# First attention stage: V's projection behind the penalties, product with V one slot later, earlier reciprocals, an end without slots

## The chip, the cores and the metric

The kernel runs on one NeuronCore of a Trainium2 chip. Its engines work side by side, each through its own queue in order: TensorE (PE in the profile; its weight loads are PEld), VectorE (DVE), ScalarE (ACT), GpSimd (POOL) and SyncE (SP), which issues most of the transfers. They wait for each other by semaphores. PE writes its results to PSUM, from where DVE or ACT copy them to SBUF.

The metric is the device time of one execution in microseconds (us). Before the change the median of three runs is 2411.57 us (2407.48 to 2413.13).

## The reference

The input is x, 4 sequences of 512 tokens with 128 features, all in float32. The first stage, the only one that the change touches, is one causal attention layer with 16 heads of 64; `x` here has gone through a layernorm without weights, and the result is added to the input:

```python
q = (x @ Wq).reshape(b, s, HEADS, HEAD_DIM)
k = (x @ Wk).reshape(b, s, HEADS, HEAD_DIM)
v = (x @ Wv).reshape(b, s, HEADS, HEAD_DIM)
scores = SCALE * jnp.einsum('bqhd,bkhd->bhqk', q, k)
causal = jnp.triu(jnp.ones((s, s), dtype=x.dtype), k=1)
scores = scores + MASK_PENALTY * causal
attn = jax.nn.softmax(scores, axis=-1)
out = jnp.einsum('bhqk,bkhd->bqhd', attn, v).reshape(b, s, HEADS * HEAD_DIM)
return out @ Wr
```

The penalty is -50, not minus infinity, so every score counts. The second stage is a second layernorm and six layers of windowed attention and a gated feed-forward block; its result is added too.

## The kernel before

Everything is kept transposed: features on the 128 partitions, the 512 tokens of a sequence along the free axis. The second stage starts at about 631 us of the profiled execution and isn't touched.

The first stage goes through 128 "rows" (class `Rows`): for each sequence `b` (4), each pair of heads `c` (8, as `NC`), and each tile `t` of 128 queries (4). The order of the instructions is the order in which the program issues them (`manual_schedule`). A loop over *slots* `m` (L321) handles two rows per slot, so two slots, an even and an odd one, make one pair of heads. A slot works on `now`, its two rows, and on `old`, the two rows of the slot before. For a row:

- `scores` (L216): 8 matmuls of Q by K into a PSUM tile `sc` of two banks; there are two such tiles, so a row takes the one that the same row of the last slot had.
- `penalty` (L229): adds the mask to the tile by a matmul with an identity in bf16.
- `maximum` (L241, DVE): the negated row maxima of both heads.
- `exponents` (L247, ACT): two activations that also give the row sums `den`; they read `sc` and so set it free.
- `inverse` (L256, DVE): the reciprocals of `den`, 128x2. `normalise` (L259, POOL): multiplies the probabilities by them.
- `transposes` (L270): a slot later, four PE transposes per head into a bank `pt` (two of them); head 0 is copied out by ACT (L274), head 1 by DVE (L276), to `pT1`, a tile for one pair of heads with two buffers.

Between these stand the projections. `make_q` (L180, copied out by ACT, L182) comes in even slots, `make_k` (L186, copied out by DVE, L188) in odd ones, both for the next pair of heads. `make_v` (L195, copied out by DVE, L202) makes one token tile of V for 8 heads; it stands in odd slots (28 of 32, of which slot 1 makes three, and slot 0 makes two). All of them, the layernorm steps (L93, L102, L110) and `project_out1` (L302) write the one PSUM bank `pj`, so each waits until the one before it has been copied out.

`times_v1` (L287) multiplies V by the transposed probabilities of one pair of heads, in two halves of four matmuls, into the one bank `o1`; after the second half DVE copies it out (L297, `aT`). In the kernel before, slot `m` begins with a half for the pair `(m - 3) // 2`: the first half in odd slots, the second in even ones. The probabilities that the first half reads were transposed and copied in the slots up to the one just before.

`project_out1` (L302, 8 matmuls, added to the input by DVE in L303) of a sequence follows in the second slot pair of the next sequence. The layernorm steps of the next sequence (`norm_x`: mean, var, scale) and of the stage's results (`norm_x1`) are put at the end of 18 of the even slots. The var step ends in a chain of small DVE operations (L104, L79 to L85).

The last slots run with no rows: the loop goes to `last + 5`, that is 64 slots with rows and 5 that hold only what is left (transposes, products with V, the last output projection).

Of the kernel before, what the change touches and what calls it, by code (L numbers as in the profile page):

```python
# [20 lines left out]
NC = INNER // P  # L21
# [10 lines left out]
def body(ctx: ExitStack, tc: tile.TileContext, a, out: bass.AP):  # L32
# [7 lines left out]
    B, S, _ = x.shape  # L40
    L = a["wqkv"].shape[0]
    NT = S // P
# [79 lines left out]
    def norm_x1(bank, b):  # L122


        def out_():
            xT[b] = new_xT()
            return xT[b]

        return layernorm_steps({}, bank, lambda: x1T[b], out_)


    with tc.tile_pool(name="s1", bufs=1) as s1, tc.tile_pool(
# [20 lines left out]
        def bank1():  # L153
            return ps1.tile([P, 512], F32, tag="pj", name="ps_pj", bufs=1)
# [13 lines left out]
        def norm_x(b):  # L168
            def out_():
                xnT[b] = s1.tile([P, S], F32, tag="xnT", name="xnT", bufs=2)  # L170
                return xnT[b]

            return layernorm_steps({}, bank1, lambda: x0T[b], out_)
# [16 lines left out]
        def make_v(b, j, t):  # L190

            if t == 0:
                vs[b, j] = s1.tile([P, NT, 512], F32, tag="v1", name="v1", bufs=3)
            p = bank1()
            mm(  # L195
                p,
                lhsT=xnT[b][:, t * P : (t + 1) * P],
                rhs=wv[:, j * 512 : (j + 1) * 512],
                start=True,
                stop=True,  # L200
            )
            nc.vector.tensor_copy(vs[b, j][:, t, :], p)  # L202
# [75 lines left out]
        def times_v1(b, c, half):  # L278

            if half == 0:  # L280
                os_[b, c] = ps1.tile([P, S], F32, tag="o1", name="ps_o1", bufs=1)
            o = os_[b, c]
            for k in (2 * half, 2 * half + 1):
                for h in range(2):
                    col = (2 * c + h) % HEADS * HD
                    j, col = col // 512, col % 512
                    mm(  # L287
                        o[h * HD : (h + 1) * HD, :],
                        lhsT=vs[b, j][:, k, col : col + HD],
                        rhs=pTs[b, c][:, h, k, :],  # L290
                        start=(k == 0),
                        stop=(k == NT - 1),
                        skip_group_check=True,
                    )
            if half == 1:
                at = aTs[b, c] = s1.tile([P, S], F32, tag="aT1", name="aT1", bufs=NC + 2)
                nc.vector.tensor_copy(at, o)  # L297

        def project_out1(b):
            y = bank1()  # L300
            for c in range(NC):
                mm(y, lhsT=wr[:, c, :], rhs=aTs.pop((b, c)), start=(c == 0), stop=(c == NC - 1))  # L302
            nc.vector.tensor_tensor(x1T[b], y, x0T[b], ALU.add)  # L303
# [12 lines left out]
        make_k(0, 0)  # L316

        last = len(rows) // 2  # L320
        for m in range(last + 5):  # L321
            b, c, odd = m // (2 * NC), m // 2 % NC, m % 2
            now = rows[2 * m : 2 * m + 2]
            old = rows[2 * m - 2 : 2 * m] if m else []

            g = (m - 3) // 2
            if 0 <= g < B * NC:
                times_v1(g // NC, g % NC, 1 - odd)
            for r in now:
                r.scores()  # L330
            for r in now:
                r.penalty()
            if now:
                now[0].maximum()
            if old:
                old[0].transposes()
            if now:
                now[0].exponents()
                now[1].maximum()

            bn, cn = (b, c + 1) if c + 1 < NC else (b + 1, 0)
            if bn < B:
                (make_k if odd else make_q)(bn, cn)
            if old:
                old[1].transposes()
            if now:
                now[1].exponents()
                now[0].inverse()
                now[0].normalise()
            if m < 2:  # L350
                make_v(0, 0, 2 * m)
                make_v(0, 0, 2 * m + 1)
            if odd and c < NT and b < B:
                make_v(b, 1, c)
            elif odd and c >= NT and b + 1 < B:
                make_v(b + 1, 0, c - NT)
            if now:
                now[1].inverse()
                now[1].normalise()
            if not odd and 1 <= c <= 3 and b + 1 < B:  # L360
                if c == 1:
                    norms[b + 1] = norm_x(b + 1)
                norms[b + 1][c - 1]()
            if b > 0 and c == 1 and odd:
                project_out1(b - 1)
                norms1[b - 1] = norm_x1(bank1, b - 1)
            if b in range(1, B) and not odd and 4 <= c <= 6:
                norms1[b - 1][c - 4]()


    s2 = ctx.enter_context(tc.tile_pool(name="s2", bufs=1))
# [518 lines left out]
```

## Time and profile before

| what | value |
|---|---|
| median of three runs | 2411.57 us |
| the profiled execution as timed | 2416.6 us |
| its span, first to last instruction | 2414.8 us |
| first score matmul of slot 0 | 27.21 us |
| end of the last output projection of the first stage | 630.6 us |
| mean granted PE clock | 0.992 |
| PE busy from 300 to 400 us | 89.48 us of 100 |
| DVE, ACT, POOL busy there | 56.49, 43.65, 38.01 us |

The span is taken in the same profiled execution as the rows that the prediction uses. PE is the engine that is busy longest in both stages. A row of the timeline gives the start in us, the length in us, the engine, the line and operation, the tile written and the tiles read, and in square brackets the idle time of the engine just ahead of it with what ended it. Matmuls of float32 count twice in the number of instructions (128x512 x2 is one projection). Matmuls are pipelined, so the next one often starts before the row's end.

### The profile page before, as it was taken

To read this page: it belongs to the slowest core of one execution; us is meant where nothing else is said; L and a number is where in the kernel's file an instruction comes from. 1 tells how busy PE (TensorE), PEld (TensorE's weight loads), DVE (VectorE), ACT (ScalarE), POOL (GpSimd) and SP (SyncE) were. 2 spreads that over 40 slices of the span, in tenths; PEclk is the share of its full clock that TensorE was granted. 3 is DMA by queue.
4 is the path that set the end of the run, shared out by engine and by line. 5 is a ranking of instruction groups with operands and counts; after the bars stand their busy time and mean duration, and the time that the engine had idled before them with its cause. 6 is when DMAs were issued, how large, how long until landed. Compare 5 with 4: busy or idle time off the path is not lost.

```text
span 2414.8 us, 81635 instructions
## 1 busy us (share of the span) xinstructions
PE 2230.5 (92%) x35056; PEld 1446.4 (60%) x35088; DVE 1697.1 (70%) x2692; ACT 1300.6 (54%) x2166; POOL 1435.9 (59%) x1897
## 2 busy tenths in 40 slices
PE   6888989889788999999999999999999999999997
PEld 3555555555356666666666666666666666666664
DVE  3655555646577777777777777778787777877874
ACT  2444444445244655656665555665556656655662
POOL 1443443434476767667767667677667677666660
PEclk9999999999899999999999999999999999999999
DMA  3000000000122233222332223222232223322220
GB/s 108 1 1 1 1 1 1 1 1 1 36 59 65 57 85 78 55 71 61 86 73 58 68 62 85 68 66 64 65 88 63 65 69 78 81 59 67 65 58 15
DMA packets 91027, 125.82 MB, mean 52 GB/s; under 512 B 25263, under 2 KB 39469, under 8 KB 90669
## 3 DMA queue, kind: packets, MB, share of 16 engines
q1 hardware_dynamic: 90236, 119.02, 20.1%
q8 instruction: 280, 4.59, 0.9%
q10 hardware_dynamic: 432, 1.57, 0.2%
q14 instruction: 79, 0.64, 0.1%
HBM read 20.41 MB, written 1.05 MB: 9 GB/s over the span
## 4 chain that ended last, share of the span: by engine, by line
PE 58%; DVE 11%; issue 3%; ACT 2%; POOL 0%; ACTq 0%; POOLq 0%
PE ps_proj L436 19%; PE ps_one L532 10%; PE ps_one L627 7%; PE ps_att L602 6%; PE ps_att L570 5%; PE ps_proj L660 2%; PE ps_proj L661 2%; PE ps_proj L674 2%; DVE on L612 2%; DVE yt L79 1%; DVE rot L457 1%; DVE t L461 1%; ACT vt L514 1%; PE ps_att L559 1%; PE ps_one L93 1%
## 5 line engine op out<-in xcount | busy, mean ns | idle before, releaser
L436 PE MATMUL ps_proj<-wqkv,xs 128*128 128x512 f32 x1152 | 570.5, 618 | 31.6 <-ACT vt L514 22.9
L472 POOL TENSOR_TENSOR rot<-rot,t 128x1024 f32<-128x1024 f32 x192 | 453.4, 2361 | 196.8 <-DVE t L461 194.9
L259 POOL TENSOR_TENSOR pr<-pr,den 128x1024 f32<-128x1024 f32 x128 | 239.9, 1894 | 375.5 <-DVE den L256 375.5
L447 ACT ACTIVATE sq<-ps_proj 128x1024 f32<-128x1024 f32 x192 | 196.9, 1025 | 408.5 <-PE ps_proj L436 370.5
L480 POOL TENSOR_TENSOR rot<-rot,ss 128x1024 f32<-128x1024 f32 x192 | 365.4, 1903 | 15.1
L436 PEld LDWEIGHTS ps_proj<-wqkv,xs 128*128 128x128 f32 x1152 | 199.5, 191 | 219.9 <-issue 157.3
L452 DVE TENSOR_REDUCE ss<-sq 128x16 f32<-128x1024 f32 x192 | 233.1, 1214 | 54.0 <-ACT sq L447 53.2
L241 DVE TENSOR_REDUCE nm<-ps_sc 128x2 f32<-128x1024 f32 x128 | 156.0, 1219 | 124.4 <-PE ps_sc L229 124.4
L274 ACT COPY pT<-ps_pt 128x512 f32<-128x512 f32 x128 | 75.1, 587 | 300.6 <-PE ps_pt L270 300.6
L457 DVE TENSOR_TENSOR rot<-ps_proj,lt 128x1024 f32<-128x1024 f32 x192 | 233.5, 1216 | 0.0
L461 DVE TENSOR_TENSOR t<-ps_proj,lt 128x1024 f32<-128x1024 f32 x192 | 232.9, 1213 | 0.0
L627 PEld LDWEIGHTS ps_one<-aT,wo 128*128 128x128 f32 x1536 | 186.3, 192 | 45.3 <-issue 44.5
L82 POOL TENSOR_TENSOR yt<-y 128x32 f32<-128x32 f32 x288 | 69.3, 241 | 241.5 <-DVE y L80 226.5
L532 PE MATMUL ps_one<-ident,rot 128*128 128x128 f32 x1536 | 211.2, 281 | 1.2 <-ACT qT L535 0.6
L580 DVE TENSOR_REDUCE mx<-ps_att 128x16 f32<-128x1024 f32 x96 | 117.5, 1224 | 120.2 <-PE ps_att L570 120.2
L247 ACT ACTIVATE pr<-ps_sc,nm 128x512 f32<-128x512 f32 x256 | 175.2, 696 | 23.1 <-DVE nm L241 23.0
L627 PE MATMUL ps_one<-aT,wo 128*128 128x128 f32 x1536 | 187.3, 275 | 0.4 <-ACT aT L535 0.4
L532 PEld LDWEIGHTS ps_one<-ident,rot 128*128 128x128 f32 x1536 | 165.8, 142 | 20.4 <-issue 2.8
L611 DVE RECIPROCAL rden<-ps_att 128x8 f32<-128x8 f32 x192 | 39.5, 206 | 195.9 <-PE ps_att L602 190.8
L602 PEld LDWEIGHTS ps_att<-vw,pT 64*32 64x32 f32 x9216 | 105.3, 105 | 109.4 <-issue 76.6
L602 PE MATMUL ps_att<-vw,pT 64*32 64x65 f32 x9216 | 129.9, 224 | 37.8 <-DVE on L612 28.2
L514 ACT COPY vt<-ps_proj 128x512 f32<-128x512 f32 x192 | 103.1, 589 | 85.6 <-PE ps_proj L436 84.6
(127 smaller groups left out, 4063.5 us busy)
## 6 DMA issues: line engine op xcount, KB each, us to landing
vw<-vt SPq DMA_DIRECT2D x1152, 65.0 KB
vw_first<-vt SPq DMA_DIRECT2D x336, 65.0 KB
wqkv<-in_wqkv_dram SPq DMA_DIRECT2D x18, 512.0 KB
wo<-in_wo_dram SPq DMA_DIRECT2D x6, 512.0 KB
w<-in_w_dram SPq DMA_DIRECT2D x6, 341.0 KB
xr<-in_x_dram SPq DMA_DIRECT2D x4, 256.0 KB
out_dram<-tmp_t SPq DMA_DIRECT2D x4, 256.0 KB
w<-in_w_dram SPq DMA_DIRECT2D x12, 64.0 KB
```

The lines of the kernel that those rows point to most:

```text
L247: nc.scalar.activation(self.pr[:, h, :], self.sc[:, h, :], AF.Exp, bias=self.nm[:, h : h + 1], accum_out=self.den[:, h : h + 1],)
L259: nc.gpsimd.tensor_tensor(self.pr, self.pr, self.den.unsqueeze(2).to_broadcast([P, 2, S]), ALU.mult)
L436: mm(p[:, c, :], lhsT=u.xs[:, u.T * P : (u.T + 1) * P], rhs=wpart[j][:, c * 512 : (c + 1) * 512], start=True, stop=True,)
L447: nc.scalar.activation(u.sq, u.p[j], AF.Square)
L452: nc.vector.tensor_reduce(u.ss[:, j * HEADS : (j + 1) * HEADS], heads(u.sq), AX.X, ALU.add)
L457: nc.vector.tensor_tensor(heads(t0), heads(pf), lt[:, u.T, 2 * j].unsqueeze(1).to_broadcast([P, HEADS, HD]), ALU.mult)
L461: nc.vector.tensor_tensor(t1.rearrange("p (h t d) -> p h t d", t=2, d=half), pf.rearrange("p (h t d) -> p h t d", t=2, d=half)[:, :, ::-1, :],
L472: nc.gpsimd.tensor_tensor(u.r[j], u.r[j], u.t1, ALU.add)
L480: nc.gpsimd.tensor_tensor(heads(u.r[j]), heads(u.r[j]), u.ss[:, j * HEADS : (j + 1) * HEADS].unsqueeze(2).to_broadcast([P, HEADS, HD]), AL ...
L532: nc.tensor.transpose(tp[:, c * P : (c + 1) * P], src[:, (4 * g + c) * P : (4 * g + c + 1) * P], ident)
L602: mm(o[j * W : (j + 1) * W, h, c * (HD + 1) : (c + 1) * (HD + 1)], lhsT=u.pT[h * HD : (h + 1) * HD, 4 * g + c, j * W : (j + 1) * W], rhs=u ...
L627: mm(y[:, 0:P], lhsT=wo_w[0][:, c, :], rhs=u.aT[:, c, :], start=(c == 0), stop=(c == NC - 1))
```

## The change

It reorders the loop and nothing else; every instruction of the first stage is still issued, as often as before.

```diff
-        for m in range(last + 5):
+        for m in range(last + 1):
...
-            g = (m - 3) // 2
-            if 0 <= g < B * NC:
-                times_v1(g // NC, g % NC, 1 - odd)
+            if m >= 4:
+                g = m // 2 - 2
+                times_v1(g // NC, g % NC, odd)
             for r in now:
                 r.scores()
             for r in now:
                 r.penalty()
             if now:
                 now[0].maximum()
+            if m < 2:
+                make_v(0, 0, 2 * m)
+                make_v(0, 0, 2 * m + 1)
+            if odd and c < NT:
+                make_v(b, 1, c)
+            elif odd and b + 1 < B:
+                make_v(b + 1, 0, c - NT)
             if old:
                 old[0].transposes()
...
             if bn < B:
                 (make_k if odd else make_q)(bn, cn)
+            if now:
+                now[0].inverse()
+                now[0].normalise()
             if old:
                 old[1].transposes()
             if now:
                 now[1].exponents()
-                now[0].inverse()
-                now[0].normalise()
-            if m < 2:
-                make_v(0, 0, 2 * m)
-                make_v(0, 0, 2 * m + 1)
-            if odd and c < NT and b < B:
-                make_v(b, 1, c)
-            elif odd and c >= NT and b + 1 < B:
-                make_v(b + 1, 0, c - NT)
-            if now:
                 now[1].inverse()
                 now[1].normalise()
...
+        times_v1(B - 1, NC - 2, 1)
+        for half in range(2):
+            times_v1(B - 1, NC - 1, half)
+        project_out1(B - 1)
```

- V's projection is issued behind the penalties of the slot's two rows, ahead of the transposes and of K's projection. The bank `pj` then goes from Q (slot before) to V to K; before, it went from Q to K to V. On DVE the copy of V moves to directly behind the first row's maximum, ahead of the copy of the first row's transposes.
- The halves of the product with V come one slot later: the first half in even slots, the second half, and with it the copy L297, in odd ones.
- The first row's reciprocal and normalisation are issued ahead of the second old row's transposes. On DVE that puts the reciprocal ahead of that row's copy L276.
- The five slots without rows become one (for the last transposes), and what is left of the products with V and the last output projection is written out behind the loop.

## The prediction

> **What bounds the kernel now.** I began with the page: busy shares, then the 40 slices. The first stage fills the first ten slices (up to about 625 us of 2414.8); only there does the change reorder work.
>
> ```profile
> PE 2230.5 (92%) x35056; PEld 1446.4 (60%) x35088; DVE 1697.1 (70%) x2692; ACT 1300.6 (54%) x2166; POOL 1435.9 (59%) x1897
> ...
> PE   6888989889788999999999999999999999999997
> ```
>
> TensorE (PE) is the busiest engine, and in the first stage its digits are mostly 8 and 9: no room but its own waits. So the second view is what PE waited for between 60 and 600 us (columns: engine, tile and line <- releaser: us in all, times, longest).
>
> ```profile
> PE ps_pj L195 <- DVE k L188: 25.5, 27, 1.1
> PE ps_o L287 <- ACT pT L274: 10.7, 12, 0.9
> PE ps_pt L270 <- DVE pT L276: 6.2, 6, 1.0
> PE ps_sc L229 <- issue: 4.6, 29, 0.2
> ...
> PE ps_pj L302 <- DVE v L202: 2.3, 3, 0.8
> ```
>
> Two waits carry it: V's projection (L195) for K's copy out of the single `pj` bank, in 27 odd slots; and the product with V (L287) for the ScalarE copy of the last transpose, in 12 even slots. The third view is the timeline of one odd slot (from 94.10) and one even slot (from 102.98).
>
> ```profile
> 94.10 2.00 PE L216 MATMUL ps_sc<-k,q 64*128 64x256 f32 x16
> ...
> 96.37 1.04 PE L270 MATMUL ps_pt<-ident,pr 128*128 128x128 f32 x8
> ...
> 96.46 1.22 DVE L241 TENSOR_REDUCE nm<-ps_sc 128x2 f32<-128x1024 f32 x1 [2.18 <-PE ps_sc L229]
> ...
> 97.25 1.02 PE L186 MATMUL ps_pj<-xnT,wk 128*128 128x512 f32 x2
> ...
> 98.11 1.04 PE L270 MATMUL ps_pt<-ident,pr 128*128 128x128 f32 x8
> ...
> 99.33 0.68 DVE L188 COPY k<-ps_pj 128x512 f32<-128x512 f32 x1
> ...
> 100.06 1.13 PE L195 MATMUL ps_pj<-wv,xnT 128*128 128x512 f32 x2 [0.92 <-DVE k L188]
> ...
> 101.12 1.94 PE L287 MATMUL ps_o<-pT,v 128*64 128x512 f32 x8
> ...
> 102.98 2.00 PE L216 MATMUL ps_sc<-k,q 64*128 64x256 f32 x16
> ...
> 107.42 1.04 PE L270 MATMUL ps_pt<-ident,pr 128*128 128x128 f32 x8
> ...
> 108.69 0.59 ACT L274 COPY pT<-ps_pt 128x512 f32<-128x512 f32 x1
> ...
> 109.34 1.08 PE L287 MATMUL ps_o<-pT,v 128*64 128x512 f32 x4 [0.89 <-ACT pT L274]
> ```
>
> Read starts: K's projection ends at 98.27, yet its copy starts at 99.33, because VectorE (DVE) is busy with a maximum; L195 is held to 100.06. An odd slot with V takes 102.98 - 94.10 = 8.88 us. Scores follow L287 by 1.87 (101.12 to 102.98), so the even slot ends at 111.21: 8.23 us.
>
> **The change, part by part.** Times below count from a slot's first score matmul.
>
> *V's projection behind the penalties (27 odd slots after the first pair).* No instruction is added. Without V and without a wait an odd slot takes 6.85 (timeline: L216 at 591.89, L270 594.16, L186 595.04, L270 595.90, L287 596.87, L216 598.74). One projection takes the queue 0.86 (L186 to L270). So: V at 2.27, first transposes 3.15, K 4.03, second transposes 4.9, product 5.9, next scores 7.72 if nothing waits. K now needs V's copy out of the bank. DVE: row maximum 2.36 to 3.58; the next DVE work starts 1.14 after a maximum starts (302.81 to 303.94), so V's copy runs 3.50 to 4.18 (0.68; V itself ends at 3.39); a PE consumer follows a copy's end by 0.05 (99.33 + 0.68 to 100.06). K starts at 4.24: a wait of 0.21 takes the place of 0.92. The slot takes 7.94, a gain of 0.94. Queued behind K are the second transposes and the next slot. Bounds: wait 0 (gain 1.16) to 0.92 (gain about 0.25); I take 0.21 since every duration in it has a row.
>
> The transposes come 0.88 later, and ScalarE (ACT) copies them before its exponents: copy 3.75 to 4.34, first row's exponents to 5.8 (1.45 each row), second row's 6.26 to 7.7. The next slot's second row of scores, which needs that PSUM back, starts at 7.94 + 0.95: 1.2 us cover. GpSimd (POOL) normalises 6.9 to 10.65 (3.75 for two rows); the next slot transposes these rows at 10.6 and 12.4, while they are ready at 8.8 and 10.65: 1.8 us cover.
>
> Of these 27 slots five follow a slot that computes a variance, whose chain of small operations holds DVE:
>
> ```profile
> 75.13 1.82 DVE L80 TENSOR_SCALAR y<-yt 128x4 int32<-128x4 int32 x1
> ...
> 79.25 1.22 DVE L241 TENSOR_REDUCE nm<-ps_sc 128x2 f32<-128x1024 f32 x1
> ```
>
> L80 takes 0.17 at 13.16, where POOL is idle, and 1.82 here: it ends at 76.95 as POOL's normalisation does (73.18 + 3.75). The maximum starts at 3.78 instead of 2.36. After the change the early reciprocal lets POOL end 0.33 sooner, but the copy of the finished product (L297, 0.60) moves into odd slots, ahead of the maximum: maximum 4.13, V's copy ends 5.94, K 6.0, second transposes 6.86, next scores 9.59, against 10.30 before (75.47 to 85.77). Gain 0.71. Three slots go on to the output projection (L302): it waited 0.78 for V's copy, and will wait about as long for K's (K ends 5.26, copy 5.97 to 6.65). Before, scores to scores 16.81 (197.34 to 214.15); after 6.7 + 7.06 + 1.87 = 15.63, gain 1.18.
> Sum: 19 x 0.94 + 5 x 0.71 + 3 x 1.18 = 25.0.
>
> *Product with V one slot later.* The two buffers of transposed probabilities allow it: the second half is issued ahead of the transposes that refill its buffer. In 12 even slots without a layernorm step L287 then follows the second transposes by 0.97 (595.90 to 596.87) rather than 1.92 (107.42 to 109.34): 12 x 0.95 = 11.4. The last even slot (598.74 to 606.84) gains about 1.1. In the 18 slots with a layernorm step that step hid the copy: nothing. Bounds: 10.7 (PE's listed wait alone) to 12.5; I take 12.5, as starts include the weight reload.
>
> *Early reciprocals.* An instruction of 0.15 is moved ahead of a copy; if it must wait, the copy L276, the second reciprocal and the next maximum queue behind it. Even slot (scores at 307.60): DVE ends the second maximum at 5.59 (311.97 + 1.22), the sums are ready at 5.34 (312.74 + 0.20): cover 0.25. Odd: 6.6 against 5.8. So it costs nothing; without cover it delays DVE, not yet PE, whose transposes need that bank 3 us later. What POOL gains lies behind its 2 us of cover, except the 0.33 above.
>
> *Start and end.* Slots 0 and 1 issue two and three V projections in a row, each waiting for the copy before it, and the second maximum queues behind these copies. The second row's exponents end at about 50.3, K's copy at 49.2; slot 2 scores at 49.3 and 50.4 (before 49.05 and 50.0), slot 3 at 56.4 (before 57.85), since it has no product yet. That 1.4 gain is owed at the end: one more product half (1.94) behind the last transposes, and a wait of about 0.85 for L297 that slots used to hide, with all of the projection queued behind it; POOL starts 0.5 sooner. I get 16.8 to 18.5 from the last slot's scores to L302 (before 606.85 to 623.46 = 16.61), middle a loss of 1.0. In the four last odd slots, without V, the one behind a variance loses 0.3. Together 0; bounds -2 and +2.
>
> **Sum:** 25.0 + 12.5 = 37.5 us. The profiled execution: 2414.8 span (2416.6 as timed) becomes 2377.3 (2379.1). It lies 5 us above the median shown, 2411.57, which becomes 2374.
>
> **Rivals.**
> *The wait only moves (0.20).* `pj` stays a single bank, written by Q or K and V in turn. If V's copy comes 0.7 later than I place it (another DVE item ahead), K waits 0.9: 27 x 0.7 = 19 of the 37.5 go, time 2393. For: the maximum stands directly ahead of that copy. Against: V is ready at 3.39, before the maximum is done.
>
> *The clock holds (0.10).* Two of the six slots behind a variance lost half of PE's clock.
>
> ```profile
> 284.00:286.00 2.00, 0.81 (x5) 0.95 0.00 0
> 286.00:288.00 2.00, 2.00 (x4) 0.50 0.00 0
> ```
>
> (Columns: window, length, PE busy and count, granted clock, DMA.) There two waits of 1.04 and 1.07 came within 3 us, and the stretch at half clock after such waits cost 1.65 (L195 + L287 take 1.19 + 3.52 at 230.26, 1.13 + 1.94 at 100.06). With one wait of 1.8 in their place these may go, and one at the end: 3.3 to 5, time about 2370.
> The Trainium skill (TensorE: Matmul & The Clock Gate, "What's actually happening") has the clock fall after an idle window of about 3.4 us; here 2.1 us of waits in pieces were enough, so the rows are stricter than that rule. By the rule alone no slot would fall, and the time would be about 2370.
>
> *The clock falls in every odd slot: slower (0.04).* If K's new wait, with what follows it, reaches some 2.1 us in 4, each of 27 odd slots pays 1.65: 45 lost against 37.5 won, time 2419. It decides from the point at which 23 of 27 fall. Against: 22 such slots with a wait of 0.92 kept a granted clock of 1.00, and I count 0.21.
> The skill's same page ("A second HAM failure mode: psum-queue depth-cycling") tells of such small idles between PSUM banks making the clock swing; it speaks against this change, but the trace's ordinary odd slots, with longer waits of that kind, don't show it.
>
> *It doesn't do what it says (0.04).* Another wait of the same size ends last in each slot, such as the second row's scores for their PSUM (cover 1.2 in odd and 0.6 in even slots): gain near 0, time 2411. Nothing in the listed waits points there.
>
> **How the numbers follow.** Forecast 0.62, the others as above. What the measurement can tell from no change is about 0.2%, 5 us. Faster: 0.62 + 0.20 + 0.10 = 0.92; the "no" case gives same 0.03 and, with the falling clock, slower 0.05. The range runs from 2364 (every wait bound at its best, the clock whole, and 4 us of spread between runs) to 2394 (the moved wait).
>
> **What would show it.** L195 should wait for nothing in the steady slots, and L186 appear waiting for the V copy L202 with about 0.2 each, some 5 in all. L287's wait for L274 should be gone from the even slots. Odd slots of 7.9 and even ones of 7.3, 15.2 a pair against 17.1. L256 should wait no longer for L247 than before. Wrong: L186's waits near 0.9, scores waiting for exponents (L247), or granted clocks of 0.5 in ordinary odd slots.

## The result, and the profile after

The changed kernel takes 2372.97 us (median of 4 runs, 2370.81 to 2376.22) against 2412.35 us (4 runs, 2407.48 to 2417.58): ratio 0.9838, 95% interval 0.9814 to 0.9861. The forecast was 2374, its range 2364 to 2394. The profiled execution has a span of 2371.3 us, 43.5 less than before. At the addition that ends the first stage (L303) 39.7 of these have been won: 630.63 before, 590.91 now. The other 3.8 came about in the second stage, which isn't touched; the four runs of either kernel differ by more than that.

The page of the changed kernel, PE's share and its slices:

```profile
PE 2222.6 (94%) x35056; PEld 1448.1 (61%) x35088; DVE 1696.8 (72%) x2692; ACT 1301.6 (55%) x2166; POOL 1436.9 (61%) x1897
...
PE   6999999998789999999999999999999999999997
```

The same instructions fill more of a shorter span; the gain is in the first ten slices, where digits of 8 became 9. What PE waited for between 60 and 575 us:

```profile
PE ps_pj L186 <- DVE v L202: 9.1, 5, 1.8
PE ps_sc L229 <- issue: 4.8, 30, 0.2
...
PE ps_pj L302 <- DVE k L188: 1.5, 3, 0.5
PE ps_pt L270 <- DVE pT L276: 1.4, 1, 1.4
```

The 25.5 us of V's projection (L195) and the 10.7 of the product (L287) are gone. What came in their place is K's wait for V's copy, 9.1 us in five slots only, those behind a variance. An odd slot (from 90.28) and an even one (from 98.31) of the timeline:

```profile
90.28 2.00 PE L216 MATMUL ps_sc<-k,q 64*128 64x256 f32 x16
...
92.55 1.08 PE L195 MATMUL ps_pj<-wv,xnT 128*128 128x512 f32 x2
...
93.47 1.04 PE L270 MATMUL ps_pt<-ident,pr 128*128 128x128 f32 x8
...
93.78 0.68 DVE L202 COPY v<-ps_pj 128x512 f32<-128x512 f32 x1
...
94.52 1.13 PE L186 MATMUL ps_pj<-xnT,wk 128*128 128x512 f32 x2
...
95.48 1.04 PE L270 MATMUL ps_pt<-ident,pr 128*128 128x128 f32 x8
...
96.45 1.94 PE L287 MATMUL ps_o<-pT,v 128*64 128x512 f32 x8
...
98.31 2.00 PE L216 MATMUL ps_sc<-k,q 64*128 64x256 f32 x16
...
102.75 1.04 PE L270 MATMUL ps_pt<-ident,pr 128*128 128x128 f32 x8
...
103.71 1.94 PE L287 MATMUL ps_o<-pT,v 128*64 128x512 f32 x8
...
105.58 2.00 PE L216 MATMUL ps_sc<-k,q 64*128 64x256 f32 x16
```

K's projection starts at 4.24 in its slot (94.52 - 90.28), 0.06 after V's copy ends. The odd slot takes 8.03 us (8.88 before), the even one 7.27 (8.23 before). K's small wait isn't in the list of waits, because the modelled end of the transposes ahead of it (93.47 + 1.04) reaches up to it; only the starts show it.

Slot lengths from the starts of L216, summed over the first stage from the first score to L303 (603.42 before, 563.77 after):

| where | won, us |
|---|---|
| 19 odd slots with V, 0.855 each | 16.2 |
| 3 odd slots that go on to the output projection | 3.4 |
| 5 odd slots behind a variance: 3 x 0.46, 2.11, 2.07 | 5.6 |
| 12 even slots without a layernorm step, 0.955 each, and the last one, 1.14 | 12.6 |
| slots 0 to 2 | 2.4 |
| odd slot behind the last variance, and the end | -0.6 |
| sum | 39.6 |

### The profile page after: what moved, and what is told of

It is laid out like the page before. It is cut to its first block, busy times and chain, and to the rows that moved or that the text cites. A ratio compares the mean times of both kernels' runs of the same rounds, so it can differ in the third digit from the quotient of the medians.

```text
span 2371.3 us, 81682 instructions
## 1 busy us (share of the span) xinstructions
PE 2222.6 (94%) x35056; PEld 1448.1 (61%) x35088; DVE 1696.8 (72%) x2692; ACT 1301.6 (55%) x2166; POOL 1436.9 (61%) x1897
## 4 chain that ended last, share of the span: by engine, by line
PE 77%; DVE 14%; issue 3%; ACT 3%; POOL 1%; DMA 1%; SPq 0%; ACTq 0%; POOLq 0%
PE ps_proj L439 19%; PE ps_one L535 10%; PE ps_one L630 7%; PE ps_att L605 6%; PE ps_att L573 6%; PE ps_sc L216 5%; PE ps_o L287 4%; PE ps_pt L270 3%; PE ps_proj L663 3%; PE ps_proj L664 3%; PE ps_proj L677 2%; DVE on L615 2%; DVE yt L79 2%; ACT vt L517 1%; DVE rot L460 1%
## 5 line engine op out<-in xcount | busy, mean ns | idle before, releaser
L614 DVE RECIPROCAL rden<-ps_att 128x8 f32<-128x8 f32 x192 | 39.6, 206 | 193.5 <-PE ps_att L605 192.0
L270 PEld LDWEIGHTS ps_pt<-ident,pr 128*128 128x128 f32 x1024 | 119.2, 141 | 55.3 <-issue 44.9
```

The source lines that it names most:

```text
L270: nc.tensor.transpose(pt[:, k * P : (k + 1) * P], self.pr[:, h, k * P : (k + 1) * P], ident)
```

## The experiments

Each run was timed against the kernel before on its own chip; the ratios are to that.

**1. V's projection alone.** The kernel before, with the block of `make_v` moved up:

```diff
             if now:
                 now[0].maximum()
+            if m < 2:
+                make_v(0, 0, 2 * m)
...
             if old:
                 old[0].transposes()
```

> The kernel before with one part of the change: V's projection directly behind the penalties; the product with V, the reciprocals and the end stay. My theory (the two waits of PE are independent): odd slots with V fall from 8.88 to about 8.0 us, even slots stay at 8.22 with the 0.89 wait for the ScalarE copy; gain 24 to 27 us, time about 2386. Rival (the parts only pay together, since V behind the second transposes also hid their copies from the product): the even slots grow by what the odd ones lose, gain under 10 us, time above 2402.

Measured 2386.87 against 2415.9, ratio 0.9884 (0.9861 to 0.9907), some 28 us. What PE waited for in this kernel, 60 to 555 us:

```profile
PE ps_o L287 <- ACT pT L274: 10.6, 12, 0.9
PE ps_pj L186 <- DVE v L202: 7.1, 5, 1.4
```

The product's wait stands as it stood (10.7 before). Odd slots take 8.03, even ones 8.22. Behind a variance the slots take 9.44, better than the change's 9.84: here the product's copy (L297) stays in even slots and isn't ahead of the late maximum. None of these five slots is 1.6 longer than the others, as two were in the kernel before. These 3.3 us are about what came over the expected gain of 24 to 27.

**2. The product alone.** The kernel before, with the products one slot later and the new end.

```diff
-            g = (m - 3) // 2
...
+            if m >= 4:
+                g = m // 2 - 2
+                times_v1(g // NC, g % NC, odd)
...
```

> The kernel before with the other part: the product with V one slot later, and the end without slots; V's projection and the reciprocals stay. My theory: even slots without a layernorm step fall from 8.22 to 7.27, odd slots stay at 8.88; 13 x 0.95 = 12 us plus about 1 at the start, time about 2399. Rival (V's projection takes the place of the wait): gain under 5 us.

Measured 2400.36 against 2415.9, ratio 0.9949 (0.9929 to 0.9969), some 12 us. Even slots 7.27, odd ones 8.89. PE's waits:

```profile
PE ps_pj L195 <- DVE k L188: 25.5, 27, 1.1
PE ps_pt L270 <- DVE pT L276: 8.2, 5, 1.6
```

V's wait is what it was before. The second line grew from 1.0 to 1.6 each: it is L297 ahead of the maximum behind a variance, 0.6 per slot. Three slots ran partly at a lower granted clock here: two of the five behind a variance (12.54 and 12.36 instead of 10.90, mean granted clock 0.86), with waits of 1.64 and 1.07 a little apart, and one with the output projection (18.50 instead of 16.80, clock 0.91), whose waits were only 0.92 and 0.78.

In ordinary slots the two parts are independent, as the expectations had it: each leaves the other's wait as it was, and the rivals in which each part only pays with the other are out. Behind a variance they are not: L297 in odd slots makes K's wait longer (1.42 in run 1, 2.02 in run 3). The two gains (1.16% and 0.51%) add up to 1.67%, near the change's 1.62% and 1.64%, but the change also has the early reciprocals; both parts without these, the kernel of runs 3 and 4, gain 1.39% and 1.33%. That difference is about as wide as the intervals; its place is seen in the slots behind a variance, next.

**3 and 4. Without the early reciprocals, twice, and the changed kernel again.** The changed kernel, with the first row's reciprocal and normalisation back behind the second row's exponents:

```diff
-            if now:
-                now[0].inverse()
-                now[0].normalise()
             if old:
                 old[1].transposes()
             if now:
                 now[1].exponents()
+                now[0].inverse()
+                now[0].normalise()
                 now[1].inverse()
```

> The changed kernel with the first row's reciprocal and normalisation put back behind the second row's exponents. My theory: they lie under GpSimd's 2 us of cover, so the slots keep 8.03 and 7.27; only the slots behind a variance get some 0.3 longer each and the end 0.5: 0 to 2 us slower than the changed kernel, 2373 to 2375. Rival (part of the gain is normalisation ending sooner, so that transposes wait less): 5 us or more slower, 2378 or more, with PE waiting for GpSimd in ordinary slots.

Measured 2379.54, ratio 0.9861 (0.9836 to 0.9885): more than I had expected. Every ordinary slot is as in the changed kernel (8.03, 7.27), with no wait of PE for GpSimd listed between 60 and 560 us. So the rival had the size and not the mechanism. But two of the five slots behind a variance took 11.67 instead of 9.84, the other three 10.04. To see whether that repeats, this kernel and the changed one ran again together:

> The changed kernel again, beside the others on one chip. My theory: ratio to the kernel before 0.984, slots of 8.03 and 7.27. On the clock: the wait of 1.83 us behind a variance is short enough, so none of the five slots loses the clock again (9.84 each). Rival (the fall is a matter of luck at any wait of 1 to 2 us): one or more of the five are 1.6 us longer this time.

> The changed kernel without the early reciprocals again (wait behind a variance 2.02 us instead of 1.83; in its first profile two of five such slots were 1.63 longer). My theory: one to three of the five lose the clock again, so 1 to 5 us over the 1.6 that the slots themselves cost; 2 to 6 us slower than the changed kernel on this chip. Rival: no such slot falls, and the two kernels differ by under 2 us.

The changed kernel: 2373.28, ratio 0.9836 (0.9808 to 0.9863). Without early reciprocals: 2380.47, ratio 0.9867 (0.9841 to 0.9894). The two intervals overlap, but on this one chip the six runs of each kernel don't (2368.6 to 2376.39 against 2378.23 to 2382.89). Four of the five slots were long this time, more than the one to three expected. The windows of three of these slots without early reciprocals (columns: window, length, PE busy and count, granted clock, DMA share, GB/s):

```profile
73.30:84.98 11.68, 9.65 (x50) 0.85 0.00 0
211.04:222.75 11.71, 9.69 (x50) 0.85 0.00 1
...
410.14:420.18 10.04, 8.02 (x51) 1.00 0.00 0
```

and of two in the changed kernel's second run:

```profile
72.97:82.81 9.84, 8.02 (x50) 1.00 0.00 0
208.88:218.72 9.84, 8.02 (x51) 1.00 0.01 2
```

The long slots are those in which the granted clock fell. Where it falls is seen in the timeline of the first of them:

```profile
79.55 1.12 PE L186 MATMUL ps_pj<-xnT,wk 128*128 128x512 f32 x2 [2.03 <-DVE v L202]
80.51 1.67 PE L270 MATMUL ps_pt<-ident,pr 128*128 128x128 f32 x8
82.11 2.94 PE L287 MATMUL ps_o<-pT,v 128*64 128x512 f32 x8
```

After K's wait of 2.03 the transposes take 1.67 instead of 1.04 and the product 2.94 instead of 1.94. With early reciprocals the wait is 1.83, and none of ten such slots fell in two profiles; with 2.02 to 2.03 six of ten did.

**5. V's projection behind the first transposes.** The changed kernel, with the moved block of `make_v` (not that of slots 0 and 1) a place lower:

```diff
-            if odd and c < NT:
-                make_v(b, 1, c)
...
             if old:
                 old[0].transposes()
+            if odd and c < NT:
+                make_v(b, 1, c)
...
```

> The changed kernel with V's projection behind the first old row's transposes instead of ahead of them (slots 0 and 1 keep their first V projections where the change has them). My theory (K starts 0.05 after V's copy, and VectorE takes that copy up behind maximum and transposes' copy): K at 5.0 instead of 4.24 in a slot, 22 x 0.77 + 5 x 0.6 = 20 us slower than the changed kernel, about 2393, and K's wait for V's copy listed with 0.7 or more in each odd slot. Rival (any place ahead of K does, as the bank's turn costs nothing): the same as the changed kernel, 2373.

Measured 2396.09 against 2415.9, ratio 0.9922 (0.9899 to 0.9945), by the ratios some 20 us slower than the changed kernel. PE's waits:

```profile
PE ps_pj L186 <- DVE v L202: 29.6, 27, 2.5
```

Odd slots take 8.75 instead of 8.03, and all five behind a variance, with a wait of 2.46 to 2.48, lost the clock (11.92 to 12.12). So the bank's turn does cost: this is what the rival "the wait only moves" would have looked like, 29.6 us of waiting for the same bank. One place in the queue divides it from the change.

**6. A longer wait for K.** The changed kernel, with the product's copy L297 done twice, which in ordinary slots ends ahead of the maximum:

```diff
                 nc.vector.tensor_copy(at, o)
+                nc.vector.tensor_copy(at, o)
```

> The changed kernel with the copy of the finished product (L297) done twice, on VectorE. In ordinary odd slots the second copy ends well ahead of the maximum (8.03 stays); behind a variance it adds 0.6 to K's wait: 2.4 instead of 1.83. Theory (PE's clock falls once a wait of PE grows past about 2 us): all or nearly all of the five slots lose the clock, 0.6 + 1.6 each: 12.0 instead of 9.84, 9 to 11 us slower than the changed kernel. Rival (the fall in the runs without early reciprocals came from something else there): 10.4 to 10.5 in each, 3 us slower.

Measured 2382.11 against 2410.59, ratio 0.9876 (0.9857 to 0.9896). Ordinary slots stay at 8.04. Behind a variance K waits 2.54. Two of the five:

```profile
73.68:84.24 10.56, 8.02 (x51) 1.00 0.00 0
210.29:222.49 12.20, 9.66 (x50) 0.86 0.01 1
```

Three fell (12.2), two didn't (10.56): the direction was as expected, but "all or nearly all" was too strong. With the reciprocals early and only the wait longer, the clock falls again. So the longer wait is enough, and nothing else about the reciprocals is needed; past 2 us it makes the fall likely, not certain. The odd slot behind the last variance, which has no V, agrees: there it is the transposes that wait, 2.15 in this run, and the slot lost the clock (10.79, granted clock 0.84); in the twelve other profiles they wait 0.85 to 1.63 and it did not.

**7 and 8. Copies on ScalarE.** K waits for a VectorE that is at the maximum when V is done, while ScalarE idles. So the changed kernel with V's copy on ScalarE, and then the product's copy as well:

```diff
-            nc.vector.tensor_copy(vs[b, j][:, t, :], p)
+            nc.scalar.copy(vs[b, j][:, t, :], p)
...
-                nc.vector.tensor_copy(at, o)
+                nc.scalar.copy(at, o)
```

> The changed kernel with V's copy out of the bank on ScalarE instead of VectorE. My theory (K waits for VectorE, which is at the maximum when V is done; ScalarE idles until the transposes' copy at 3.8): K at 4.07 instead of 4.24 in ordinary slots (7.86 instead of 8.03), and behind a variance no wait of K, but 0.65 for the copy of the transposes: 8.4 instead of 9.84; 22 x 0.17 + 5 x 1.4 = 11 us faster than the changed kernel. Rival (ScalarE's chain of copies and exponents is as close to the bound, so that the delayed copy of the transposes holds back the exponents and the next slot's scores): no faster, and L216 listed as waiting for L247.

> As the one before, with the copy of the finished product (L297) on ScalarE too, which in odd slots stands on VectorE ahead of the maximum. My theory: nothing in ordinary slots; behind a variance the maximum starts 0.6 sooner and the wait of 0.65 goes, 7.9 to 8.0 instead of 8.4: 3 us faster than with V's copy alone. Rival: the same, or slower as ScalarE is late for the exponents.

Measured 2361.18, ratio 0.9788 (0.9758 to 0.9818), and 2356.64, ratio 0.9767 (0.9739 to 0.9795); the changed kernel on the same chip 0.9836. So V's copy won 12.1 us over the changed kernel (11 expected) and the product's 4.5 more (3 expected). Odd slots take 7.82 in both; behind a variance they take 8.50 and then 7.90, the first of them 8.93 and 8.30. The beginning of such a slot's K in the second kernel, whose scores start at 72.81:

```profile
76.19 0.59 ACT L202 COPY v<-ps_pj 128x512 f32<-128x512 f32 x1 [2.68 <-PE ps_pj L195]
...
76.79 1.22 DVE L241 TENSOR_REDUCE nm<-ps_sc 128x2 f32<-128x1024 f32 x1
76.87 1.09 PE L186 MATMUL ps_pj<-xnT,wk 128*128 128x512 f32 x2
```

V's copy is over when VectorE has only come to the maximum, and K goes on at 4.06 in the slot without a listed wait.

**9. The fastest kernel without early reciprocals.** The edit of 3 in the kernel of 8.

> The fastest kernel so far (V's and the product's copies on ScalarE) with the early reciprocals taken back. Theory (they were worth 5 to 7 us in the changed kernel only by keeping K's wait behind a variance under the length at which the clock falls): that wait is gone here, so no slot loses the clock and it costs 0.2 in six slots and 0.5 at the end, under 2 us. Rival (sooner normalisation is worth something by itself): 5 us or more slower than with them, ratio above 0.979.

Measured 2357.61 against 2410.59, ratio 0.978 (0.9758 to 0.9802), against 0.9767 with them; the intervals overlap widely. In the profiles five slots are 0.2 longer and the end 0.6; no slot lost the clock. Where K doesn't wait, the early reciprocals are worth about 1.5 us, read from these slots.

**10. Q's copy between the exponents.** The kernel of 8; in even slots ScalarE copies Q out after the first head's exponents instead of after both.

```diff
...
-                now[0].exponents()
+                now[0].exponents((0, 1) if odd else (0,))
                 now[1].maximum()
...
                 (make_k if odd else make_q)(bn, cn)
             if now:
+                if not odd:
+                    now[0].exponents((1,))
                 now[0].inverse()
```

> The fastest kernel so far with Q's copy between the two exponents of the first row in even slots, instead of behind both. Theory (the 18 layernorm steps wait 0.41 each for Q's copy, listed with 7.1 us): that copy ends 0.6 sooner, the wait goes; the first reciprocal comes 0.4 later, which lies under cover except behind a variance, where the chain ends 0.2 to 0.4 later: 7 us won, 2 lost, 5 us faster, ratio about 0.974 to 0.975. Rival (VectorE, which must wait for the sums ahead of the copy of the transposes, hands the delay on): no gain.

Measured 2348.64 against 2410.59, ratio 0.9746 (0.9726 to 0.9766), the fastest of all. All 18 even slots with a layernorm step are 0.60 shorter by the slot starts. The price, dearer than expected: slots behind a variance are 0.7 longer, and PE's wait for the transposes' copy there, 1.1 us in all in the kernel of 8, has grown:

```profile
PE ps_pt L271 <- DVE pT L277: 4.7, 6, 1.5
```

## Why the prediction was right

**V's projection.** The mechanism and the place were as worked out: K at 4.24, with 4.24 measured. The slot was put at 7.94 and took 8.03. The difference is one step that I took from a row without a wait: from a projection to the transposes behind it 0.86, where after a wait it is 0.96 (94.52 to 95.48). Behind a variance the maximum was put at 4.13 and came at 4.18 (76.29 - 72.11), and the slot won 0.46 instead of 0.71: the same 0.1, and 0.97 instead of 0.86 from the transposes to the product. The changed kernel's rows there:

```profile
71.47 1.89 POOL L259 TENSOR_TENSOR pr<-pr,den 128x1024 f32<-128x1024 f32 x1 [0.36 <-DVE rs L104]
71.59 1.79 DVE L80 TENSOR_SCALAR y<-yt 128x4 int32<-128x4 int32 x1
...
76.29 1.22 DVE L241 TENSOR_REDUCE nm<-ps_sc 128x2 f32<-128x1024 f32 x1
...
77.42 0.68 DVE L202 COPY v<-ps_pj 128x512 f32<-128x512 f32 x1
...
78.16 1.12 PE L186 MATMUL ps_pj<-xnT,wk 128*128 128x512 f32 x2 [1.83 <-DVE v L202]
```

L80 again ends with POOL's normalisation (73.38 and 73.36). In the slot's time that is 0.20 sooner than before (9.99 against 10.19), not 0.33. That POOL holds L80 is read from such ends; no run tried it by itself.

**The product one slot later.** 12 x 0.95 and 1.1 were forecast; 12 x 0.955 and 1.14 came, and run 2 had the same with this part alone.

**Early reciprocals.** Here the prediction was wrong in size: they were costed at nothing, apart from 0.33 in five slots. Taking them back cost 0.31% (0.9836 to 0.9867), 7 us. In ordinary slots cover hides them, as I said: 8.03 and 7.27 with and without. What I left out is that 0.2 us of K's wait decides in some slots whether 1.63 more are lost to the clock. Run 9 agrees: without that wait they are worth about 1.5 us.

**Start and end.** Forecast at 0 (1.4 won, 1.0 and 0.3 lost), measured 1.85. Slot 3 began at 55.34 instead of 56.4. Of that, 0.4 is V's first projection: it took 1.02, while Q's in that place had taken 1.43 before. Where the rest comes from is not shown, and 0.6 of it is not steady: slot 0 took 9.25 here and 9.86 in the changed kernel's second profile. At the end only 0.2 was lost in place of 1.0: before, the transposes and products there ran partly at half clock (1.92 for eight transposes); after, at full (1.09).

**The rival "the clock holds"** came true beside the forecast: neither of the two slots that had fallen before did so now, 3.3 of the 39.7. The lower gain in odd slots, 1.7 us in those with ordinary waits and 1.2 behind a variance, took back about as much. With start and end the first stage won 39.7 where 37.5 was forecast; the profiled execution as a whole ended 6.0 sooner than its forecast of 2377.3, 3.8 of that in the stage that isn't touched. So part of the close agreement of 2372.97 with 2374 is chance.

**The rivals "the wait only moves" and "it doesn't do what it says"** are out by the 8.03 and 7.27; run 5 shows the first at one place's distance. **The slower rival** needed waits of about 2.1 in ordinary slots. Runs 3 to 6 show its mechanism at single waits from 2.02 on; in the change only the slots behind a variance come near that.

The Trainium skill (TensorE: Matmul & The Clock Gate, "What's actually happening") puts the fall after an idle window of about 3.4 us; here single waits of 2.02 to 2.03 and of 2.54 sufficed in 9 of 15 slots behind a variance (runs 3, 4 and 6). The free-running window that the page describes would fit a chance rather than a sharp point, but the runs don't show the window.

## What to carry to other kernels

A projection that shares one PSUM bank with others is best issued where its copy's engine is just free and other matmuls stand behind it. Walk each queue from row to row to find that place: one place lower cost 20 us here, and the copy on an engine that idles at that moment won 12 more. And a wait of PE near 2 us isn't priced by its length alone: count the half clock behind it.

## What the runs showed that I had not expected

The clock's fall after a single wait of PE has a lower edge here, in slots that are otherwise alike: 1.42 us none of 5 (run 1), 1.83 none of 10, 2.02 to 2.03 six of 10, 2.46 to 2.48 five of 5 (run 5, where V's projection comes later), 2.54 three of 5 (run 6). In these slots it begins between 1.83 and 2.02; that it grows likelier beyond is not shown. Each fall costs 1.6 us.

The length of one wait isn't the whole condition. Where two shorter waits stand close together some slots fell as well: 1.04 and 1.07 two of 5 (the kernel before), 1.64 and 1.07 two of 5 (run 2), 0.92 and 0.78 one of 6 (the output projections of both). What else decides it, no run here tells.

A reordering that moves 0.2 us under cover in all ordinary slots can so be worth 7 us.
